# Second layers of a mixture of experts as seven products for eight, with bias rows added by accumulating DMAs

## The chip, the cores and the metric

The kernel runs on one core of a Trainium2 chip. The metric is the device time of one execution in microseconds (us), lower is better. The engines are TensorE (PE in the profile, PEld its weight loads), VectorE (DVE), ScalarE (ACT), GpSimd (POOL) and SyncE (SP). SP and POOL issue the DMAs here: those of SP are in the hardware queue, those of POOL in the software queue, and only POOL's can accumulate, that is, add what they bring to what lies at the destination.

## The reference

One block on x of 2 x 512 tokens by 1024 features. Both quantised factors are rounded to eight bits, all else is float32:

```
x = x + tanh(g_xattn) * (fake_quant(layernorm(x)) @ fake_quant(ctx))      # ctx: 1024 x 1024 for each batch
n = layernorm(x)
scores = softmax(n @ router_w + router_b) + router_bias                   # 16 experts, 2 chosen for each token
z = (silu(n @ sw1 + sb1) * (n @ sw2 + sb2)) @ sw3 + sb3                   # shared expert, 512 hidden
y = sum over experts e: gate[e] * ((silu(n @ ew1[e] + eb1[e]) * (n @ ew2[e] + eb2[e])) @ ew3[e] + eb3[e])   # 256 hidden
out = x + tanh(g_ffn) * (y + z)
```

With the inputs given all tokens choose the same two experts, and the kernel has a path for at most two: there are eight chunks of 128 hidden units, four of the shared expert (chunks 0 to 3) and two of each of the two routed ones (4 to 7). A slower path for any other choice stands behind a branch and doesn't run.

The "first layers" are the products with sw1, sw2, ew1, ew2; the "second layers" the products with sw3 and ew3.

## The kernel before

A float32 product is made on PE from three products of a 32-bit format with fewer bits: each operand is split into a high part (ACT copies it into that format, L333) and a low part (DVE subtracts the high part, L334), and high x high, high x low and low x high are added up in PSUM.

The work comes in this order:
- attention, layer norm, transposes, and the shared expert's chunks 0 to 2 of the first layers, in an order written out by hand (`START`); the router (L638 to L737), whose choice is read into registers, so that weights of chosen experts can be loaded;
- chunk 3 of the shared expert and the four routed chunks (4 to 7), each in a `pair` (names s3, b4, b5, b6, b7): both first layers of a chunk over both batches, as seven products for eight (Winograd's form of Strassen's scheme, 2 x 2 blocks: the halves of the 1024 features, the two batches, the two layers). One product is twelve matmuls of 128x512. The sums of x that it needs (S1 to S4) are made once, by eight accumulating DMAs (`add_x`, L786); the differences of the weights (T's) by `prep_pair` on DVE during the pair before. After each product the caller's `between` step is issued, then what adds the product up (L430 to L452). Routed chunks are multiplied by the tokens' gates on POOL (L421), and the results go to DRAM (`h_all`, L425, POOL's queue);
- the second layers: `load_down` brings back one chunk's hidden units and weights (L862, SP), `split_down` splits them, and `down_mm` (L874, L875, L877) multiplies: for each tile of 128 tokens and each half of the 1024 output columns, all eight chunks add up in one PSUM bank. Three tiles go first, chunk by chunk as chunks arrive; then the other five one by one. x after attention was stored to DRAM (`x_after`) and comes back (`Y`, L908); DVE adds the three bias rows to it, one shared and two routed ones scaled by the tokens' gates (L912), and at last the PSUM banks (`down_end`, L916), and SP stores the tile (L917). The last tile is cut into 512, 256 and 256 columns.

From `manual.enter_context` on, each engine takes its instructions in the order of the program, and so do the two DMA queues: what waits holds up all that stands behind it on that engine or queue. Tiles come from rotating pools: 17 slabs and 14 octs, seven scratch tiles (`temp`), eight PSUM banks. A new tile waits for all users of the one whose place it takes.

Of the kernel before, what the change touches and what calls it, by code (L numbers as in the profile page):

```python
# [9 lines left out]
F32 = mybir.dt.float32  # L10
# [8 lines left out]
P = 128  # L19
D = 1024  # L20
KD = D // P
B = 2
# [57 lines left out]
def flamingo_block(  # L80
# [19 lines left out]
    def slab(name, dtype, shape=(P, D)):  # L100
        return slabs.tile(list(shape), dtype, tag="slab", name=name)
# [20 lines left out]

    X = [None] * NT
    x_after = [spill.tile([P, D], F32, name=f"x_after{t}") for t in range(NT)]
    h_all = [spill.tile([P, B * S], F32, name=f"h_all{c}") for c in range(NC)]


    dq = [nc.sync]
# [170 lines left out]
    def fn(t, h):  # L299
        nm, r = md_[t]  # L300
        nc.vector.tensor_scalar(xn_[t][:, half(h)], X[t][:, half(h)], nm, r, ALU.add, ALU.mult)  # L301
# [30 lines left out]
    def split(raw, hi, lo):  # L332
        nc.scalar.copy(hi, raw)  # L333
        nc.vector.tensor_tensor(lo, raw, hi.bitcast(F32), ALU.subtract)  # L334
        return hi, lo

    def split_in_one(name, raw):

        both = octo(name, F32R, (P, 2, *raw.shape[1:]))
        return split(raw, both[:, 0], both[:, 1])  # L340
# [37 lines left out]
    def prep_pair(name, wa, wb, W):  # L378


        lo, hi = slice(0, KH), slice(KH, KD)
        two = lambda n: tuple(slab(f"{name}{n}{m}", F32R, (P, KD, P)) for m in "hl")
        ah, al = two("a")
        W["B11"], W["B21"] = (ah[:, lo], al[:, lo]), (ah[:, hi], al[:, hi])
        t13, t24 = slab(f"{name}t13", F32, (P, KD, P)), slab(f"{name}t24", F32, (P, KD, P))
        nc.vector.tensor_tensor(t13[:, lo], wa[:, lo], wb[:, lo], ALU.subtract)
        nc.vector.scalar_tensor_tensor(t24[:, lo], t13[:, lo], -1.0, wb[:, hi], ALU.mult, ALU.subtract)
        nc.vector.tensor_tensor(t13[:, hi], wb[:, hi], wb[:, lo], ALU.subtract)
        nc.vector.tensor_tensor(t24[:, hi], wa[:, hi], t24[:, lo], ALU.add)
        split(wa, ah, al)  # L390
        yield
        b22 = slab(f"{name}b22", F32R, (P, KD, P))
        W["B22"] = split(wb[:, hi], b22[:, lo], b22[:, hi])
        yield
        for n, t in (("24", t24), ("13", t13)):
            h, l = split(t, *two(f"t{n}"))
            W[f"T{n[0]}"], W[f"T{n[1]}"] = (h[:, lo], l[:, lo]), (h[:, hi], l[:, hi])
            yield

    def pair(name, W, b1, b2, ci, gates=None, between=()):  # L400


        pa, pb, pc = (bank(f"{name}{n}") for n in "ABC")
# [17 lines left out]
                nc.gpsimd.tensor_tensor(silu, silu, gates[:, ts(b, S)], ALU.mult)  # L421

        def done(h, silu, b):
            nc.vector.tensor_tensor(h, h, silu, ALU.mult)
            nc.gpsimd.dma_start(h_all[ci][:, ts(b, S)], h)  # L425

        s1, s6, s7, s11 = (temp(f"{name}{n}") for n in ("s1", "s6", "s7", "s11"))
        product(pa, "A11", "B11", True)
# [80 lines left out]
    def sup_post(c, b, got, lo=0, n=S):  # L509
        h = up_post(f"sa{c}_{b}_{lo}", got, sb1c(c), sb2c(c), n)  # L510
        nc.sync.dma_start(h_all[c][:, b * S + lo : b * S + lo + n], h)
# [241 lines left out]
    def begin(n, raws):  # L753
        prep[0] = prep_pair(f"b{n}", *raws, W[n])
        next(prep[0])

    def go():
        next(prep[0], None)
# [2 lines left out]
    begin(3, raw3)  # L761
    go()
    go()
    sup_post(0, 1, got, 0, 256)
    go()
    lT = []
# [49 lines left out]
    load_block(SC)  # L816
    for j in range(2):
        nc.sync.dma_start(g_row[j].rearrange("(t p) -> p t", p=P), chosen[j][1])
    f = lambda fn, *a: (lambda: fn(*a))
    pair("s3", W[3], sb1c(3), sb2c(3), 3, None, (  # L820
        [f(split_x, "S1", s1)],
        [f(split_x, "S4", s4)],
        [f(lambda: begin(SC, raws_up[SC]))],
        [go],
        [go],
        [go, f(load_block, SC + 1), f(load_gates, 0)],
    ))
    down_prep = []
    for n in range(SC, NC):
        j, c = divmod(n - SC, EC)  # L830
        bv = chosen[j][2]
        if n + 1 < NC:
            between = (
                [f(begin, n + 1, raws_up[n + 1])], [], [go], [go], [go], [],
                [f(load_block, n + 2)] if n + 2 < NC else [],
            )
        else:
            between = down_prep
        if c == 0 and j == 1:
            load_gates(1)  # L840
        if n == NC - 1:
            break
        pair(f"b{n}", W[n], bv[:, 0, c : c + 1], bv[:, 1, c : c + 1], n, gates[j], between)


    def expert_row(w, e, c=None):
        if c is None:
            return w[ds(e, 1), :].rearrange("o d -> (o d)").partition_broadcast(P)
        return w[ds(e, 1), ts(c, P), :].rearrange("o p d -> (o p) d")

    def w3_rows(c):
        if c < SC:
            return sw3[ts(c, P), :]
        j, c = divmod(c - SC, EC)
        return expert_row(ew3, chosen[j][0], c)

    hid, w3, raw_down = [], [], {}

    def load_down(c):
        raw_down[c] = slab(f"h{c}r", F32), slab(f"d{c}r", F32)  # L860
        for raw, src in zip(raw_down[c], (h_all[c], w3_rows(c))):
            nc.sync.dma_start(raw, src)  # L862

    def split_down(c):
        for n, raw, got in zip("hd", raw_down[c], (hid, w3)):
            if c == 0:
                got.append(split(raw, *(slab(f"{n}{c}{m}", F32R) for m in "hl")))
            else:
                got.append(split_in_one(f"{n}{c}", raw))

    def down_mm(po, t, c, cols):
        (hh, hl), (wh, wl) = hid[c], w3[c]
        for p, cl in zip(po, cols):
            nc.tensor.matmul(p, hh[:, ts(t, P)], wh[:, cl], start=c == 0, stop=False)  # L874
            nc.tensor.matmul(p, hh[:, ts(t, P)], wl[:, cl], start=False, stop=False)  # L875
        for p, cl in zip(po, cols):
            nc.tensor.matmul(p, hl[:, ts(t, P)], wh[:, cl], start=False, stop=c == NC - 1)  # L877

    def bias_row(name, row):
        bb = slab(name, F32)  # L880
        dq[0].dma_start(bb, row)
        return bb

    n, bv = NC - 1, chosen[1][2]
    load_down(0)
    pair(f"b{n}", W[n], bv[:, 0, 1:2], bv[:, 1, 1:2], n, gates[1], (
        [f(load_down, 1)],
        [f(split_down, 0), f(load_down, 2)],
        [f(split_down, 1)],
        [f(split_down, 2), f(load_down, 3)],  # L890
        [f(split_down, 3), f(load_down, 4)],
        [f(split_down, 4), f(load_down, 5)],
        [f(load_down, 6)],
    ))

    gt = rt("gt", (P, 2, NT))
    for j in range(2):
        nc.vector.tensor_scalar(gt[:, j], chosen[j][1], tgf, None, ALU.mult)
    rows = []

    def load_rows():
        rows.append((bias_row("sb", sb3.partition_broadcast(P)), lambda t: tgf))
        for j in range(2):
            rows.append((bias_row(f"eb{j}", expert_row(eb3, chosen[j][0])), lambda t, j=j: gt[:, j, t : t + 1]))

    def down_load(t):
        X[t] = slab(f"Y{t}", F32)
        nc.sync.dma_start(X[t], x_after[t])  # L908

    def down_bias(t):  # L910
        for bb, scale in rows:
            nc.vector.scalar_tensor_tensor(X[t], bb, scale(t), X[t], ALU.mult, ALU.add)  # L912

    def down_end(po, t, cols):
        for p, cl in zip(po, cols):
            nc.vector.scalar_tensor_tensor(X[t][:, cl], p, tgf, X[t][:, cl], ALU.mult, ALU.add)  # L916
            nc.sync.dma_start(of[ts(t, P), cl], X[t][:, cl])  # L917

    halves = [half(0), half(1)]
    first, rest, last = (4, 5, 6), (7, 0, 1, 2), 3  # L920
    po = {t: [bank(f"po{t}_{h}") for h in range(2)] for t in first}
    for c in range(NC):
        if c == 0:
            split_down(5)
        if c == 1:
            load_down(7)
            split_down(6)
        if c == 2:
            split_down(7)
            load_rows()  # L930
            for t in first:
                down_load(t)
        if c == 4:
            for t in first:
                down_bias(t)
        for t in first:
            down_mm(po[t], t, c, halves)
    for t in first:
        down_end(po[t], t, halves)
    order = (*rest, last)  # L940
    for t in order[:2]:
        down_load(t)
    for n, t in enumerate(rest):
        down_bias(t)
        po = [bank(f"po{t}_{h}") for h in range(2)]
        for c in range(NC):
            down_mm(po, t, c, halves)
        down_end(po, t, halves)
        if n + 2 < len(order):
            down_load(order[n + 2])  # L950
    down_bias(last)
    for cl in (slice(0, 512), slice(512, 768), slice(768, 1024)):
        po = [bank(f"po{last}_{cl.start}")[:, : cl.stop - cl.start]]
        for c in range(NC):
            down_mm(po, last, c, [cl])
        down_end(po, last, [cl])
    manual.close()


# [47 lines left out]
                xl(t, h)  # L1007

    def mlp(name, n, up, down, b1, b2, row, scale):
        bb = bias_row(f"{name}bias", row)  # L1010
        for t in range(NT):
            nc.vector.scalar_tensor_tensor(X[t], bb, scale(t), X[t], ALU.mult, ALU.add)
        for c in range(n):
# [97 lines left out]
```

## Time and profile before

| what | before |
|---|---|
| time, median of 3 (lowest, highest) | 322.97 us (322.70, 323.48) |
| profiled execution: its own time, its span | 323.01 us, 321.3 us |
| granted PE clock, mean | 0.994 |
| pair b7 begins | 208.61 us |
| first matmul of the second layers | 228.24 us |
| last addition on DVE begins | 316.30 us |
| DMA: moved, mean rate over the span | 53.44 MB, 166 GB/s |
| of that hardware queue, software queue | 46.27 MB, 6.82 MB |
| accumulating DMAs (L786) | 8 of 512 KB |

Times inside the profile count from the span's start. "Share" of DMA is the mean busy share of the core's 16 DMA engines. A group "L916 DVE ... xcount" is all instructions of one line and shape, with their mean duration. The chain of waits names, going back from the last instruction, what ended last at each step.

### The profile page before, as it was taken

The page shows a single profiled execution, that of the slowest core. Times are in us where ns is not written, and L with a number is a line of the kernel's source. Part 1 is how long each engine was busy: PE and PEld are TensorE (multiplying, and loading weights), DVE is VectorE, ACT ScalarE, POOL GpSimd, SP SyncE. Part 2 cuts the span into 40 slices and gives each one's busy share as a digit, 9 for nine tenths or more (in the row PEclk, how much of TensorE's full clock was granted, in tenths as well). Part 3 has the DMA queues.
Part 4 walks back from the last instruction along what each step waited for, and adds up shares of the span by engine and source line. Part 5 has one row for each costly group of instructions (what it writes and reads, how often), then busy time and mean ns, then how long its engine had stood idle before and what let it go on. Part 6 is the DMA issues. An engine that isn't in the chain of part 4 may idle for free.

```text
span 321.3 us, 4424 instructions
## 1 busy us (share of the span) xinstructions
PE 306.1 (95%) x1626; PEld 244.9 (76%) x1631; DVE 218.8 (68%) x360; ACT 116.2 (36%) x176; POOL 88.7 (28%) x130
## 2 busy tenths in 40 slices
PE   8588799999999999999999999999999999999993
PEld 2244695869995988888888888887788888888883
DVE  3869999997476886396657546479762975663261
ACT  2666669676545307361323324057610000000000
POOL 2695678896900322000013131112200000000000
PEclk9799999999999999999999999999999999999999
DMA  6999992029210999246341604459569053332121
GB/s 207 421 380 358 418 313 111 2 81 343 68 34 18 179 184 208 77 94 149 115 128 66 192 36 149 147 196 337 208 210 356 5 195 131 132 131 74 59 98 41
DMA packets 35105, 53.44 MB, mean 166 GB/s; under 512 B 5436, under 2 KB 23172, under 8 KB 35076
## 3 DMA queue, kind: packets, MB, share of 16 engines
q1 hardware_dynamic: 33124, 46.27, 42.0%
q0 software_dynamic: 1952, 6.82, 8.7%
q8 instruction: 15, 0.25, 0.3%
q14 instruction: 14, 0.11, 0.1%
HBM read 36.29 MB, written 12.59 MB: 152 GB/s over the span
## 4 chain that ended last, share of the span: by engine, by line
PE 83%; DVE 4%; DMA 4%; POOL 4%; issue 2%; ACT 2%; SPq 0%; DVEq 0%; POOLq 0%
PE sp L549 11%; PE sp L360 10%; PE po L877 9%; PE po L874 9%; PE po L875 9%; PE at L251 5%; PE b4B L410 3%; PE b6B L410 3%; PE b5B L410 3%; PE s3B L410 3%; DMA h4r<-h_all 2%; DMA X<-in_dram 2%; PE px L306 2%; PE b7A L410 2%; PE b5C L410 2%
## 5 line engine op out<-in xcount | busy, mean ns | idle before, releaser
L875 PE MATMUL po<-d,h 128*128 128x512 f32 (+1 forms) x119 | 44.9, 377 | 0.0
L874 PE MATMUL po<-d,h 128*128 128x512 f32 (+1 forms) x119 | 44.9, 377 | 0.0
L877 PE MATMUL po<-d,h 128*128 128x512 f32 (+1 forms) x119 | 36.9, 377 | 0.0
L251 PE MATMUL at<-cq,qT 128*128 128x512 bf16 x123 | 29.7, 379 | 2.9 <-POOL cq L170 1.7
L916 DVE SCALAR_TENSOR_TENSOR Y<-po,tg,Y 128x512 f32<-128x512 f32 (+1 forms) x17 | 11.4, 715 | 21.4 <-PE po L877 21.3
L875 PEld LDWEIGHTS po<-d,h 128*128 128x128 f32 x119 | 22.4, 188 | 4.1
L874 PEld LDWEIGHTS po<-d,h 128*128 128x128 f32 x119 | 22.4, 188 | 4.1
L877 PEld LDWEIGHTS po<-d,h 128*128 128x128 f32 x119 | 22.4, 188 | 4.1
L251 PEld LDWEIGHTS <-qT 128*128 128x128 bf16 x128 | 12.1, 97 | 15.7 <-issue 3.0
L912 DVE SCALAR_TENSOR_TENSOR Y<-eb,gt,Y 128x1024 f32<-128x1024 f32 x16 | 20.6, 1285 | 0.6
L912 DVE SCALAR_TENSOR_TENSOR Y<-sb,tg,Y 128x1024 f32<-128x1024 f32 x8 | 10.2, 1278 | 10.3 <-DMA Y<-x_after 10.3
L786 POOL DMA_DIRECT2D xf<-xf x8 | 7.2, 931 | 28.8 <-PE plt L649 15.0
L549 PE MATMUL sp<-XH,sb 128*128 128x256 f32 x96 | 14.1, 292 | 0.0
L549 PE MATMUL sp<-XH,sa 128*128 128x256 f32 x96 | 13.7, 288 | 0.0
L316 DVE TENSOR_TENSOR XL<-px,XH 128x512 fp32r<-128x512 f32 x16 | 10.4, 678 | 3.7 <-ACT xf L323 3.7
L549 PEld LDWEIGHTS sp<-XH,sb 128*128 128x128 f32 x96 | 12.3, 191 | 0.5 <-DVE sb L164 0.2
L360 PE MATMUL sp<-XH,sa 128*128 128x256 f32 (+1 forms) x64 | 12.5, 338 | 0.0
L360 PE MATMUL sp<-XH,sb 128*128 128x256 f32 (+1 forms) x64 | 12.5, 338 | 0.0
L549 PEld LDWEIGHTS sp<-XH,sa 128*128 128x128 f32 x96 | 12.3, 192 | 0.1
L272 ACT ACTIVATE xn<-X,s 128x512 f32<-128x512 f32 x16 | 11.4, 716 | 2.1 <-DVE X L263 1.8
L301 DVE TENSOR_SCALAR xn<-X,nm,d 128x512 f32<-128x512 f32 x16 | 11.2, 726 | 1.4 <-POOL d L297 1.3
L183 DVE BATCH_NORM_STATS2 st<-X 128x6 f32<-128x512 f32 x16 | 10.3, 680 | 2.3 <-DMA X<-in_dram 2.3
(499 smaller groups left out, 690.6 us busy)
## 6 DMA issues: line engine op xcount, KB each, us to landing
cr<-in_dram SPq DMA_DIRECT2D x15, 512.0 KB, 9.9
x_after<-X SPq DMA_DIRECT2D x8, 512.0 KB, 4.3
xf<-xf POOLq DMA_DIRECT2D x8, 512.0 KB, 5.1
Y<-x_after SPq DMA_DIRECT2D x8, 512.0 KB, 5.3
out_dram<-Y SPq DMA_DIRECT2D x15, 256.0 KB, 2.0
X<-in_dram SPq DMA_DIRECT2D x7, 512.0 KB, 9.0
h_all<-sa SPq DMA_DIRECT2D x8, 128.0 KB, 1.8
gates<-g_row SPq DMA_DIRECT2D x2, 512.0 KB, 5.3
```

The costliest lines, as they stand in the source:

```text
L251: nc.tensor.matmul(acc[t][h], qT[b][:, t % TB, k, :], cq[b][k // KH][:, k % KH, half(h)], start=(k == 0), stop=(k == KD - 1))
L272: nc.scalar.activation(xn_[t][:, half(h)], X[t][:, half(h)], AF.Square, bias=s[:, h : h + 1], scale=-float(H), accum_out=q[:, h : h + 1],)
L301: nc.vector.tensor_scalar(xn_[t][:, half(h)], X[t][:, half(h)], nm, r, ALU.add, ALU.mult)
L316: nc.vector.tensor_tensor(XL[b][q][p], px_[t, q], XH[b][q][p].bitcast(F32), ALU.subtract)
L360: nc.tensor.matmul(p, wx[:, k, :], xx[b][k // KH][:, k % KH, cols], start=first and k == 0, stop=last and k == KD - 1,)
L410: nc.tensor.matmul(p, w[:, k, :], x[:, k, :], start=f and k == 0, stop=l and k == KH - 1, skip_group_check=not first,)
L549: nc.tensor.matmul(up_[c, lo, i], w[:, k, :], x[0][k // KH][:, k % KH, lo : lo + 256], start=p == 0 and k == 0, stop=p == 2 and k == KD - 1,)
L874: nc.tensor.matmul(p, hh[:, ts(t, P)], wh[:, cl], start=c == 0, stop=False)
L875: nc.tensor.matmul(p, hh[:, ts(t, P)], wl[:, cl], start=False, stop=False)
L877: nc.tensor.matmul(p, hl[:, ts(t, P)], wh[:, cl], start=False, stop=c == NC - 1)
L912: nc.vector.scalar_tensor_tensor(X[t], bb, scale(t), X[t], ALU.mult, ALU.add)
L916: nc.vector.scalar_tensor_tensor(X[t][:, cl], p, tgf, X[t][:, cl], ALU.mult, ALU.add)
```

## The change

The second layers become one 2 x 2 block product, in seven products for eight: the hidden units are cut into shared (512) and routed (512) and into the two batches, the weights into shared and routed rows and the two halves of the columns. With `A11`, `A12` = shared and routed hidden units of batch 0, `A21`, `A22` of batch 1, and `B11`, `B12`, `B21`, `B22` the weights (shared rows first), the sums are S1 = A21 + A22, S2 = S1 - A11, S3 = A11 - A21, S4 = A12 - S2, T1 = B12 - B11, T2 = B22 - T1, T3 = B22 - B12, T4 = T2 - B21 (with a sign taken into the code: `nS3`, `nT3`, `T4` as B21 - T2). Products are made in four groups of 128 tokens, each twelve matmuls of 128x512, in the order A11 B11, A12 B21, S2 T2, nS3 nT3, A22 T4, S1 T1, S4 B22.

- The first product is needed in both batches' sums: ACT copies its PSUM banks to four others, on which later products add up.
- The sums of hidden units are made by accumulating DMAs from DRAM (`add_part`, POOL's queue) on a tile that ACT wrote; the differences of weights by DVE in place (`less`).
- After each product but the first, DVE adds its PSUM banks to `Y` (`down_add`); the 24 additions of 512 columns (the last one cut in two) are spread over six products, where before there were two of them for each tile at its end.
- Bias rows: the two routed ones are scaled and summed for each token tile and half (`sum_rows`, ACT and DVE) during pairs b4 to b6, and added to `x_after` in DRAM by 16 accumulating DMAs of 256 KB (`add_sum`, POOL). The shared row is scaled by ACT once and added to each loaded `Y` by an accumulating DMA of 512 KB (`add_row`, POOL), eight in all. DVE's 24 bias additions go.
- `done` stores hidden units through SP's queue instead of POOL's.
- `prep_pair` works in place in the raw weights and is spread over one step more.

```diff
-    h_all = [spill.tile([P, B * S], F32, name=f"h_all{c}") for c in range(NC)]
+    h_dram = [spill.tile([P, KH, B * S], F32, name=f"h{n}") for n in ("shared", "routed")]
+    h_all = [h_dram[c // SC][:, c % SC] for c in range(NC)]
...
-            nc.vector.tensor_tensor(h, h, silu, ALU.mult)
-            nc.gpsimd.dma_start(h_all[ci][:, ts(b, S)], h)
+            got = keep[0] if keep and b == 0 else h
+            nc.vector.tensor_tensor(got, h, silu, ALU.mult)
+            nc.sync.dma_start(h_all[ci][:, ts(b, S)], got)
...
+    def sum_rows(h, t):
+        u = sums[h, t] = temp(f"u{h}_{t}")
+        nc.scalar.mul(u, rows[h][:, 0], gt[:, 0, t : t + 1])
+        nc.vector.scalar_tensor_tensor(u, rows[h][:, 1], gt[:, 1, t : t + 1], u, ALU.mult, ALU.add)
+
+    def add_sum(h, t):
+        nc.gpsimd.dma_start(x_after[t][:, half(h)], sums[h, t], accum_op=ALU.add)
...
+    def add_part(name, part, *at, parts=(0, 1)):
+        for i in parts:
+            nc.gpsimd.dma_start(R[name][i], part(*at, i), accum_op=ALU.add)
...
+    def down_mm(p, t, a, b, first, cl=slice(None)):
+        for k in range(KH):
+            (ah, al), (bh, bl) = ((m[k // 2][:, k % 2] for m in (HI[n], LO[n])) for n in (a, b))
+            for i, (x, w) in enumerate(((ah, bh), (ah, bl), (al, bh))):
+                nc.tensor.matmul(
+                    p, x[:, ts(t, P)], w[:, cl], start=first and k == 0 and i == 0, stop=k == KH - 1 and i == 2,
+                    skip_group_check=not first,
+                )
+
+    def down_load(t):
+        X[t] = slab(f"Y{t}", F32)
+        nc.sync.dma_start(X[t], x_after[t])
+
+    def add_row(t):
+        nc.gpsimd.dma_start(X[t], rows["s"], accum_op=ALU.add)
+
+    def down_add(p, t, h, store, cl=None):
+        cl = half(h) if cl is None else slice(h * H + cl.start, h * H + cl.stop)
+        nc.vector.scalar_tensor_tensor(X[t][:, cl], p, tgf, X[t][:, cl], ALU.mult, ALU.add)
+        if store:
+            nc.sync.dma_start(of[ts(t, P), cl], X[t][:, cl])
...
+    def product(p, a, b, first, post, meanwhile):
+        for t, steps in zip(range(TB), meanwhile):
+            down_mm(p[t], t, a, b, first)
+            post(t)
+            for step in steps:
+                step()
+
+    high("A12", parts=two)
+    low("A12", parts=two)
+    scaled("S2", "nS3", 1.0)
+    add_part("S2", h_part, 1, 1)
+    for t in range(TB):
+        down_load(t)
+        add_row(t)
...
+    product(pa, "A11", "B11", True, lambda t: nc.scalar.copy(pb[t], pa[t]), (
...
+    fetch("A22", h_part, 1, 1)
+    fetch("S1", h_part, 0, 1)
+    add_part("S1", h_part, 1, 1)
+    product(pa, "A12", "B21", False, lambda t: down_add(pa[t], t, 0, True), (
+        [f(high, "S2"), f(low, "S2", parts=one)],
+        [f(low, "S2", parts=two), f(scaled, "S4", "S2", -1.0), f(add_part, "S4", h_part, 1, 0)],
...
+    product(pb, "S2", "T2", False, lambda t: down_add(pb[t], t, 1, False), (
...
+    for t in range(TB, NT):
+        down_load(t)
+        add_row(t)
+    fetch("B22b", w3_part, 1, 1)
+    product(pb, "nS3", "nT3", False, lambda t: down_add(pb[t], TB + t, 1, False), (
+        [f(low, "T4", parts=two)], [f(high, "A22"), f(low, "A22", parts=one)], [f(low, "A22", parts=two)],
+        [f(high, "S1"), f(low, "S1", parts=one)],
+    ))
+    product(pb, "A22", "T4", False, lambda t: down_add(pb[t], TB + t, 0, True), (
...
+    product(pc, "S1", "T1", True, lambda t: down_add(pc[t], TB + t, 1, True), (
...
+    product(pc, "S4", "B22b", False, lambda t: down_add(pc[t], t, 1, True), [[]] * (TB - 1))
+    for cl in (slice(0, 256), slice(256, 512)):
+        down_mm(pc[TB - 1][:, cl], TB - 1, "S4", "B22b", False, cl)
+        down_add(pc[TB - 1][:, cl], TB - 1, 1, True, cl)
```

`fetch` loads a block through SP, `high` and `low` make its two parts (ACT and DVE), `scaled` multiplies a block by a number on ACT. Operands of the first two products are loaded and split in the steps of pair b7.

## The prediction

> **What bounds the kernel now.** I read the page's busy table first, then the chain of waits in order of time, then busy time by stretches, and last the transfers. The profiled execution took 323.01 us with a span of 321.3, so 1.7 us lie around the span; the median is 322.97, so its profile stands for the median. A difference under about 0.3% (1 us) can't be told from no change here.
>
> ```profile
> PE 306.1 (95%) x1626; PEld 244.9 (76%) x1631; DVE 218.8 (68%) x360; ACT 116.2 (36%) x176; POOL 88.7 (28%) x130
> ```
> ```profile
> 208.61 2.72 PE b7A L410 x12
> 211.33 2.72 PE b7B L410 x12
> ...
> 231.12 0.61 DVE b7s L452
> ...
> 231.77 0.50 PE po L874
> ...
> 316.30 0.48 DVE Y L916
> ```
> ```profile
> 109.00:111.55 2.55, 2.55 (x18) 2.33 (x18) 2.21 (x12) 0.00 (x0) 0.86 (x1) 1.00 0.98 193
> 111.55:115.75 4.20, 4.20 (x21) 3.46 (x20) 3.79 (x13) 0.00 (x0) 0.86 (x2) 1.00 1.03 204
> 245.00:247.00 2.00, 2.00 (x11) 1.65 (x10) 0.00 (x0) 0.00 (x0) 0.00 (x0) 1.00 1.03 418
> 227.60:321.30 93.70, 88.46 (x412) 73.77 (x410) 51.44 (x53) 6.61 (x7) 2.41 (x3) 1.00 0.35 129
> 10.00:14.00 4.00, 2.82 (x10) 1.22 (x11) 3.50 (x7) 3.25 (x5) 3.39 (x8) 0.57 1.03 421
> ```
> TensorE (PE) is the bound. In the chain, a product of the first layers is twelve 128x512 matmuls in 2.72 us, 0.227 us each, and pairs follow one another every 19.04 us. The second layers run from 228 to 316 with nothing late but a 0.2 us wait at 231.77 for DVE. In the stretches (columns: bounds, length, busy us of PE, PEld, DVE, ACT, POOL, then PE clock, DMA share, GB/s) the second layers use DVE little over half and DMA 0.35. The first two stretches hold the eight accumulating transfers of L786: 512 KB each, alone, they fill the DMA engines (0.98, 1.03) at 193 to 204 GB/s. The third holds plain loads: the engines are as full at 418. So an accumulating transfer costs the engines twice a plain one: 2.6 us per 512 KB against 1.3 (at 200 and 400 GB/s).
>
> **The change, part by part.**
>
> *TensorE.* Before: 8 chunks x 8 token tiles x 2 halves x 3 = 384 matmuls. After: 7 products x 4 tiles x 12 = 336. 28 groups of twelve at 2.72 are 76.2 us, and some 0.2 for the last group cut into 256 columns. b7 begins at 208.61 and has seven products, so the second layers can begin at 227.65 and end at 304.0; the last DVE addition then starts at 304.2 instead of 316.30. If nothing waits, that is 12.1 us less: 310.9 us.
>
> *DVE, ACT.* Gone are 24 bias additions of 1.28 us on DVE; PE never waited for them, so they give nothing. New are, per product, four additions of 0.75 (L916), four low parts of 1.22 (L334) and up to two differences of some 1.2: 7.9 to 10.3 us of a product's 10.88. It fits, but DVE runs in order: one operand that comes late stops the low parts behind it. ACT has four high parts of 1.05 a product, the four PSUM copies and sums. The PSUM-to-PSUM copy has no row; PSUM to SBUF took 0.59 (L430), so 0.3 to 1.2, I take 0.6. By the order on ACT they run at 234 to 242, and the second product's first group overwrites the first copied bank from 238.5; nothing is late by either end. In the pairs, 16 sums of routed rows add 0.69 on DVE and 0.6 on ACT each, at most six a pair: DVE goes from 12.0 (its rows of pair b5) to some 16 of 19.04. The new order of `prep_pair` has the same operations one product later, finished before the next pair. Cost 0 for these.
>
> *Queues.* The ten hidden-layer stores move from POOL to SP, where what is behind waits too: the Y0 load stands behind b7's last store. That waits for: product 6's end at 224.93, addition 0.69, silu 0.72, gate 1.30, multiply 0.69, one low part 1.22, addition and multiply 1.38, near 231. Y0 to Y3 and 2 MB of hidden rows (A22, S1) leave SP from 231.4, some 0.4 us apart. On POOL the accumulations of S2 go at 233 (after two ACT parts), then the row additions of Y0 to Y3, S1, S4, then Y4 to Y7: each in this order.
>
> *DMA, where I see the loss.* From 232 the engines have work without a gap. Product 4 adds to Y4 to Y7, and each addition waits for its accumulated row. On DVE, Y6's addition stands ahead of the second low part of A22, and product 5's first group needs that at its ninth matmul. Unstalled, product 5 begins at 227.65 + 4 x 10.88 = 271.2 and that matmul at 273.0; less 1.22 and 0.75, Y6's row must have landed at 271.0. Ahead of it and with it are:
> - accumulating: S2, S1, S4 1 MB each, Y0 to Y6 0.5 each: 6.5 MB x 5.24 us = 34.1;
> - plain: Y0 to Y7 4 MB, A22 and S1 2, four half tiles stored 1, the last weights (B22b) 1: 8 MB x 2.62 = 21.0.
>
> Together 55.1 us from 232, and some 1.2 from the last byte to the wait's end (transfers of L786, issued in pairs, landed 4.5 to 6.5 us after issue): 288.3. The order between the two queues hardly matters, as the plain ones have all been issued by 262. Then 0.75 and 1.22, and four matmuls more: the group ends at 291.2 against 273.9, 17.3 late. Earlier waits (product 3 for S2's low part behind Y1's row, some 3 us) are inside that. PE has then stood nearly idle from 274 to 290. At the start, where it had waited 2.93 us, the granted clock was 0.57 over 4 us (last stretch): 4 x 0.43 = 1.7 more. Sum: 310.9 + 17.3 + 1.7 = 329.9, say 330.
>
> *The unknown prices.* S2, S1 and S4 accumulate from DRAM in 2 KB pieces; the trace has accumulation from SBUF in 4 KB pieces only. I take the same 2.6 per 512 KB, the nearest row. As cheap as plain copies, 3 MB come 7.9 cheaper: 322.0. Half as dear again: 337.8. The routed sums accumulate into DRAM (16 x 256 KB, no such row): 1.3 each by that row, 21 us over three pairs whose DMA share is about half; I take 0 for their delay. At three times that, b7's scratch tiles, which wait for the accumulation issued near 209, would hold PE up to 5 us. A gain here I exclude: nothing was waiting.
>
> *What the Trainium skill says.* "DMA: Bandwidth & Descriptors", section "Anatomy of one DMA — SWDGE (gpsimd) path", fits any transfer from GpSimd as 2.0 us and its bytes at 436 GB/s, without a word on accumulation. By it the 6.5 MB would be an estimated 15.6 us of engine time, the sum 36.6 after 232, Y6 in time, and the change worth its 12.1 us. The stretches at 193 to 204 GB/s speak against it, and I go by them. Against the change speaks the same page's section "Queues, rings and completion order": an engine takes its queues in turn, packet by packet, so that plain and accumulating packets would wait for each other; no row of this trace has the two together for long.
>
> **Rivals.**
> 1. *Faster: plain copies ride inside accumulations.* If an accumulating packet only waits for its second read, the engine could move plain packets meanwhile. Place: the same wait of DVE for Y4 to Y7. Up to 271.0 there are 271.0 - 232 - 1.2 = 37.8 us for 34.1 of accumulation, so it decides at 3.7 us: with no more than that charged for the 21.0 of plain copies, product 5 waits for nothing, and it is 310.9; with half charged, 6.8 late, some 318. For it: the mix is not in the trace. Against it: shares of 0.98 and 1.03 in both kinds, never the sum of two. 310.9 to 319.
> 2. *Near no change: accumulation from DRAM at the plain price.* 322.0 as above, 319 to 324 with the landing times. Against it: an accumulation reads two operands wherever they lie, and 200 is half of 400.
> 3. *Slower still: accumulation into DRAM holds the pairs* (b5 to b7), as priced: 335 to 342. For it: no row shows this kind. Against it: at the price taken, its 21 us of engine time have three pairs, 57 us, to fit in.
>
> That the change doesn't do what it says I set aside: the order of PE's instructions shows the 336 matmuls.
>
> **How the numbers follow.** Forecast (late row additions, near 330; own range 323 to 337): 0.62. Rival 1: 0.23. Rival 2: 0.10. Rival 3: 0.05. Faster is rival 1 and half of rival 2: 0.28. Same is 0.04, from rival 2's middle; slower the rest, 0.68. The range must take in most of rival 1 as well: 313 to 337; it leaves out rival 3's far half, the edges, and rival 1's unstalled end.
>
> **What would show it.** Right: PE's products at 2.72 us per group; DVE waiting for Y's rows with software transfers as releaser, longest before product 5's operands; PE nearly idle for over 10 us between products 4 and 5; DMA share near 1 from 232 to 288 with 250 to 300 GB/s; a clock under 1 after it. Wrong: PE without a wait through 28 groups (rival 1), a first wait of DVE for Y0 under 1 us, or PE waits inside b6 or b7 (rival 3). A span under 316 refutes the DMA sum; products at another pace than 2.72 refute the first term.

## The result, and the profile after

The changed kernel takes 343.86 us (median of 4, 342.40 to 345.49); the kernel before, beside it, 323.23. The ratio is 1.0639, interval 1.0583 to 1.0694: slower by 6.4%. Medians are of all executions; the ratios and their intervals leave out those over 1.5% above the kernel's fastest. The forecast was slower, near 330.0 and at most 337: the direction held, the size did not. The profiled execution took 342.40 us with a span of 340.6, 12.5 us more than the forecast.

The busy table of the kernel after:

```profile
PE 303.9 (89%) x1566; PEld 239.5 (70%) x1571; DVE 231.9 (68%) x380; ACT 147.7 (43%) x215; POOL 113.8 (33%) x152
```

PE has 60 instructions less than before, but is busy for 2.2 us less only, and its share falls from 95% to 89%. So it waits, and what it does takes longer. The waits of PE (us in total, times, longest), those of the second layers:

```profile
PE pb L921 <- DVE Y L935: 7.1, 1, 7.1
PE pb L921 <- DVE S2l L904: 5.2, 2, 4.1
...
PE pa L921 <- ACT pb L1003: 3.7, 1, 3.7
PE pb L921 <- DVE A22l L904: 2.8, 1, 2.8
```

The chain of waits from pair b7 on (start, length, what):

```profile
210.56 2.72 PE b7A L412 x12
...
236.50 1.30 POOL b7s L423
...
248.60 15.48 DMA Y<-rows
...
264.84 1.23 DVE S2l L904
...
266.11 6.04 PE pb L921 x16
...
272.41 10.07 DMA Y<-x_after
...
283.03 14.56 DMA Y<-rows
...
298.35 1.23 DVE A22l L904
...
299.62 13.18 PE pb L921 x46
312.80 20.48 PE pc L921 x96
```

Pair b7 begins 2 us late. Its second gate runs at 236.50. The shared row's accumulation into Y, alone 2.6 us of engine time, takes some 15 us from issue to landing, twice in the chain. DVE adds to Y only then, and makes the low parts of S2 and A22 behind that. Product 5 goes on in the PSUM banks of product 4, so its first matmul waits until the addition to Y4 has read its bank: this is the longest wait, 7.1 us. From 299.62 on PE waits for 0.6 us only.

Busy time by stretches (bounds, length, then PE, PEld, DVE, ACT, POOL, then granted clock, DMA share, GB/s): the second layers from their first matmul to the last addition, the end of b6 and b7, and the stretch of the late rows:

```profile
229.72:335.60 105.88, 86.32 (x349) 68.63 (x347) 56.53 (x61) 30.15 (x33) 15.53 (x15) 0.87 0.75 202
205.00:232.00 27.00, 27.00 (x120) 22.04 (x119) 15.07 (x17) 10.79 (x13) 9.51 (x10) 1.00 1.04 279
240.00:297.60 57.60, 40.70 (x150) 31.17 (x148) 30.28 (x31) 21.69 (x25) 14.24 (x14) 0.83 1.03 266
```

The DMA engines are full (1.03) from 240 to 297.6, as forecast for 232 to 288, but they were full before that too: 1.04 from 205 to 232, where the forecast had room. In the first line PE is busy for 86.32 us on work of 76.4 (28 groups at 2.72 us and the cut of the last), at a clock of 0.87.

### The profile page after: what moved, and what is told of

Same layout as the page of the kernel before. It is cut to its first block, busy times and chain, and to the rows that moved or that the text cites. A ratio compares the mean times of both kernels' runs of the same rounds, so it can differ in the third digit from the quotient of the medians.

```text
span 340.6 us, 4476 instructions
## 1 busy us (share of the span) xinstructions
PE 303.9 (89%) x1566; PEld 239.5 (70%) x1571; DVE 231.9 (68%) x380; ACT 147.7 (43%) x215; POOL 113.8 (33%) x152
## 4 chain that ended last, share of the span: by engine, by line
PE 51%; DMA 25%; issue 10%; SPq 5%; DVE 4%; POOL 2%; ACT 2%; POOLq 0%; DVEq 0%; ACTq 0%
PE sp L552 10%; DMA Y<-rows 9%; PE sp L364 8%; PE pc L921 7%; PE pb L921 6%; DMA cr<-in_dram 5%; DMA e0a1r<-in_dram 4%; PE at L252 4%; DMA Y<-x_after 3%; DMA x_after<-u 2%; PE px L307 2%; PE b6B L412 2%; PE b4B L412 2%; PE b5A L412 2%; PE b7A L412 2%
## 5 line engine op out<-in xcount | busy, mean ns | idle before, releaser
L935 DVE SCALAR_TENSOR_TENSOR Y<-pb,tg,Y 128x512 f32<-128x512 f32 x12 | 9.0, 749 | 18.9 <-DMA Y<-rows 16.3
L853 POOL DMA_DIRECT2D x_after<-u x16 | 14.0, 949 | 10.5 <-DVE u L850 10.5
L423 POOL TENSOR_TENSOR b4s<-b4s,gates 128x512 f32<-128x512 f32 x2 | 2.8, 1396 | 43.9 <-ACT b4s L439 36.3
L849 ACT ACTIVATE u<-row,gt 128x512 f32<-128x512 f32 x16 | 11.3, 721 | 9.1 <-DMA x_after<-u 6.1
L892 POOL DMA_DIRECT2D rS<-hrouted x6 | 7.3, 1505 | 22.1 <-DMA rS<-hshared 14.9
L935 DVE SCALAR_TENSOR_TENSOR Y<-pc,tg,Y 128x512 f32<-128x512 f32 (+1 forms) x9 | 6.2, 691 | 11.7 <-PE pc L921 11.7
L921 PE MATMUL pb<-T4h,A22h 128*128 128x512 f32 x16 | 7.6, 473 | 7.1 <-DVE Y L935 7.1
L552 PE MATMUL sp<-XH,sa 128*128 128x256 f32 x96 | 13.7, 287 | 0.0
L850 DVE SCALAR_TENSOR_TENSOR u<-row,gt,u 128x512 f32<-128x512 f32 x16 | 11.7, 746 | 1.3 <-ACT u L849 1.0
L364 PE MATMUL sp<-XH,sa 128*128 128x256 f32 (+1 forms) x64 | 12.5, 338 | 0.0
L364 PE MATMUL sp<-XH,sb 128*128 128x256 f32 (+1 forms) x64 | 12.5, 337 | 0.0
L921 PE MATMUL pb<-T2h,S2l 128*128 128x512 f32 x16 | 7.6, 473 | 5.2 <-DVE S2l L904 5.2
```

The costliest lines, as they stand in the source:

```text
L364: nc.tensor.matmul(p, wx[:, k, :], xx[b][k // KH][:, k % KH, cols], start=first and k == 0, stop=last and k == KD - 1,)
L552: nc.tensor.matmul(up_[c, lo, i], w[:, k, :], x[0][k // KH][:, k % KH, lo : lo + 256], start=p == 0 and k == 0, stop=p == 2 and k == KD - 1,)
L849: nc.scalar.mul(u, rows[h][:, 0], gt[:, 0, t : t + 1])
L850: nc.vector.scalar_tensor_tensor(u, rows[h][:, 1], gt[:, 1, t : t + 1], u, ALU.mult, ALU.add)
L853: nc.gpsimd.dma_start(x_after[t][:, half(h)], sums[h, t], accum_op=ALU.add)
L921: nc.tensor.matmul(p, x[:, ts(t, P)], w[:, cl], start=first and k == 0 and i == 0, stop=k == KH - 1 and i == 2, skip_group_check=not first,)
```

## The experiments

Theory A, from the prediction: accumulating transfers fill the DMA engines, Y's rows land late, and DVE, in order, holds the operands behind them. Theory B: the loss is made before the second layers, by the routed sums. Beside each group the kernel before ran on the same chip, at 323.2 to 323.5 us.

### Which accumulations cost what

**No shared row.** `add_row` does nothing.

```diff
-        nc.gpsimd.dma_start(X[t], rows["s"], accum_op=ALU.add)
+        pass
```

> Leaves the shared bias row out of the output: the eight 512 KB accumulations into Y are gone, all else stays. Theory A (the row accumulations fill the DMA engines, so Y and the operands behind it on DVE come late): 4 MB at 5.24 us/MB = 21 us of engine time go, PE's 19 us of idle time between 240 and 306 us nearly vanish; what stays is the late start (the gate of b7 at 236.5 instead of 226.5): 317 to 324 us. Theory B (the loss is made before b7 ends, by the routed sums that hold the loads of A12 and the scratch tiles): over 332 us.

Measured: 322.14 us, ratio 0.9938 [0.9906, 0.9969]; 21.7 less than after. Theory A's value. Its longest waits in the second layers are 3.1 us for the PSUM copy and 1.5 for S2's high part: the late start is still there (gate of b7 at 238.81).

**No routed sums.** `add_sum` does nothing.

```diff
-        nc.gpsimd.dma_start(x_after[t][:, half(h)], sums[h, t], accum_op=ALU.add)
+        pass
```

> Leaves the routed bias rows out of the output: the sixteen 256 KB accumulations into x_after in DRAM are gone, their sums on ACT and DVE stay, all else stays. Theory A: b7 begins 1 to 2 us sooner, A12 lands before its high part is due, Y0 to Y3 leave SP about 10 us sooner, but the 55 us of engine time from 232 us on stay: about 330 us, the price worked out before. Theory B: under 322 us.

Measured: 334.72 us, ratio 1.0351 [1.0306, 1.0396]; 9.1 less than after. Between the two, nearer to A: B alone falls, but these transfers, taken at no delay in the prediction, cost 9.1 us. This kernel is the case that the prediction's sum described; Y's loads leave SP from 232.19 here. PE's waits, and DVE's additions to Y4, Y5 and Y6 behind the accumulated rows:

```profile
PE pb L921 <- DVE Y L935: 9.5, 1, 9.5
PE pb L921 <- DVE S2l L904: 4.7, 2, 3.3
...
PE pb L921 <- DVE A22l L904: 2.7, 1, 2.7
```
```profile
285.74 0.75 DVE L935 SCALAR_TENSOR_TENSOR Y<-pb,tg,Y 128x512 f32<-128x512 f32 x1 [14.08 <-DMA Y<-rows]
...
288.62 0.75 DVE L935 SCALAR_TENSOR_TENSOR Y<-pb,tg,Y 128x512 f32<-128x512 f32 x1 [0.99 <-DMA Y<-rows]
...
291.09 0.75 DVE L935 SCALAR_TENSOR_TENSOR Y<-pb,tg,Y 128x512 f32<-128x512 f32 x1 [0.59 <-DMA Y<-rows]
```

The sum had the row of Y6 landed at 288.3; its addition starts at 291.09, and in the kernel after at 300.35.

**Neither.** Both edits.

> Leaves all bias rows out of the output: neither the sixteen accumulations into x_after nor the eight into Y. The seven products alone, with the sums of hidden rows by DMA left. If the PE term of the prediction holds (28 groups of 2.72 us from 227.65 us): 311 to 314 us. If the sums of hidden rows (3 MB accumulating) or the order on ACT and DVE hold PE by themselves: over 317 us.

Measured: 312.87 us, ratio 0.9691 [0.9633, 0.9749]; 31.0 less than after, where the two single losses add up to 30.8. The stretch of its second layers, with the columns as above:

```profile
226.56:303.90 77.34, 76.72 (x349) 63.68 (x347) 54.68 (x59) 27.86 (x30) 7.77 (x7) 1.00 0.70 206
```

PE is busy for 76.72 of 77.34 us: the seven products, with the sums of hidden units, the PSUM copy and DVE's additions beside them, are worth 10 us against the kernel before. The bias rows cost 31, and so take back three times that.

### Engine time or order

**The row copied, not added.** Same place, source, size and waits.

```diff
-        nc.gpsimd.dma_start(X[t], rows["s"], accum_op=ALU.add)
+        nc.gpsimd.dma_start(X[t], rows["s"])
```

> The eight row transfers into Y keep their place, source, size and waits, but copy and do not add, so that Y holds the shared row in place of x and the routed rows. Theory A (an accumulating 512 KB takes the DMA engines 2.6 us, a plain one 1.3): half of the 21 us of engine time stays; the loss without the row transfers was 21.7 us smaller, so some 11 us smaller here: 331 to 335 us. Rival (it is the order of issue and the wait for each load that cost, whatever the transfer does): within 3 us of 343.9.

Measured: 333.90 us, ratio 1.0353 [1.0305, 1.0401]: 10.0 of the 21.7 us come back with nothing changed but the addition. In the trace a packet of this transfer, 4 KB, takes 327 ns where it adds and 159 where it copies.

**The routed sums copied, not added.**

```diff
-        nc.gpsimd.dma_start(x_after[t][:, half(h)], sums[h, t], accum_op=ALU.add)
+        nc.gpsimd.dma_start(x_after[t][:, half(h)], sums[h, t])
```

> The sixteen transfers of the routed sums into x in DRAM copy and do not add, so that x is lost there; all else as after. The loss without them was 9.1 us smaller. If it is engine time (178 ns of a 2 KB accumulating packet against 84 to 89 of a plain one): about half comes back, 338 to 341 us. If it is their place in the queues and the waits for them: within 2 us of 343.9.

Measured: 336.32 us, ratio 1.0426 [1.0359, 1.0493]: 7.5 of the 9.1 come back, more than the half expected, so engine time again. Adding, they go in packets of 2 KB at 210 ns in the mean; copying, of 4 KB at 170: 1.7 us of the engines for 256 KB against 0.7. ACT now waits 3.1 us for A12, not 10.5.

**A12's parts behind b7's silu.**

```diff
-    last[5] += [f(high, "A12", parts=one), f(low, "A12", parts=one), f(fetch, "B22", w3_part, 1, 1, buf=in_slabs)]
+    last[5] += [f(fetch, "B22", w3_part, 1, 1, buf=in_slabs)]
-    last[6] += [f(high, "B21"), f(low, "B21", parts=one)]
+    last[6] += [f(high, "B21"), f(low, "B21", parts=one), f(high, "A12", parts=one)]
...
+    low("A12", parts=one)
     high("A12", parts=two)
```

> Computes everything; on ACT the high part of the first half of A12 goes behind the last silu of b7, and its low part on DVE behind b7's last multiplication. Theory A2 (the late load of A12 costs its time through the order on ACT: the silu behind it, then b7's gate, store and the Y loads, come 10 us late): the gate starts near 226.5, Y0 to Y3 leave SP near 232, and of the 9 us that the routed sums cost some 7 come back: 335 to 338 us. Rival (the DMA engines are full from 205 on, so the work only waits elsewhere): over 341 us.

Measured: 338.49 us, ratio 1.0477 [1.0444, 1.0509]: 5.4 back, just outside the 335 to 338 of theory A2 and well away from the rival. The gate of b7 on POOL, in the kernel after and then here:

```profile
236.50 1.29 POOL L423 TENSOR_TENSOR b7s<-b7s,gates 128x512 f32<-128x512 f32 x1 [13.12 <-ACT b7s L450]
```
```profile
228.74 1.29 POOL L423 TENSOR_TENSOR b7s<-b7s,gates 128x512 f32<-128x512 f32 x1 [5.38 <-ACT b7s L450]
```

So the path of the routed sums is mostly this: they fill the DMA engines in b6 and b7, A12's load takes 13 us, ACT waits for it with b7's silu behind it, and gate, store and the Y loads (which leave SP from 241.45) come some 8 us late.

**The routed rows' load later.** Its packets of 2 KB took about 1 us each from 140 to 149 us, and 84 ns elsewhere.

```diff
-        [f(split_x, "S4", s4), f(load_rows, 0)],
+        [f(split_x, "S4", s4)],
...
-        [go, f(load_block, SC + 1), f(load_gates, 0)],
+        [go, f(load_block, SC + 1), f(load_gates, 0), f(load_rows, 0)],
```

> Computes everything; the load of the first half of the routed rows moves from behind the 2,048 four-byte stores of the gates (139 us) to some 10 us later. If the slow packets (near 1 us for 2 KB) belong to the place behind those stores, the row packets fall to 0.1 to 0.2 us, other loads there crawl as in the kernel before, and b4 and b5 begin 1 to 2 us sooner: 341 to 343 us. If they belong to reading one row for 128 partitions, they stay near 1 us at the new place, and the time is the same or longer.

Measured: 344.28 us, ratio 1.0661 [1.0607, 1.0716]: no gain, where 341 to 343 was expected. The point on the packets held: the row packets fall to about 0.1 us, and weight packets of 512 B, now in that place, take 166 ns in the mean (141 to 149 us), where 27 is usual. What crawls is the place behind the four-byte stores; why it does was not tried.

### Other ways to add the rows

**The shared row on GpSimd.**

```diff
-        nc.gpsimd.dma_start(X[t], rows["s"], accum_op=ALU.add)
+        nc.gpsimd.tensor_tensor(X[t], X[t], rows["s"], ALU.add)
```

> Computes everything: the shared row is added to each Y by one 128x1024 addition on GpSimd in place of an accumulating DMA. Theory A: the DMA engines lose the same 21 us as without the row, GpSimd gets 8 x about 2.6 us (twice its 1.30 us for 128x512) of some 100 us: within 2 us of the kernel without the row. Rival (the place in GpSimd's queue, not the engine time, makes Y late: S1 and S4 wait behind Y's loads in either form): over 5 us above the kernel without the row.

Measured: 331.87 us, ratio 1.0248 [1.0158, 1.0339]: 9.7 above the kernel without the row. The size is the rival's, the reason is neither's. The lines of the weight differences on DVE (durations in ns: least, median, most) with the additions on GpSimd, and the additions themselves, then the differences in the kernel without the row:

```profile
L915 DVE TENSOR_TENSOR rB<-rB,rB x8: 1211/2288/3416, 243.7 to 274.8; 128x1024 f32<-128x1024 f32 x8
...
L931 POOL TENSOR_TENSOR Y<-Y,rows x8: 2395/3336/3397, 245.6 to 285.9; 128x1024 f32<-128x1024 f32 x8
```
```profile
L915 DVE TENSOR_TENSOR rB<-rB,rB x8: 1212/1217/1220, 246.7 to 272.6; 128x1024 f32<-128x1024 f32 x8
```

While GpSimd adds, a DVE subtraction takes up to 3.4 us for 1.2. The Trainium skill, "SBUF — State Buffer", section "Who interferes with whom", says that a DVE instruction with two inputs in SBUF contends with a GpSimd instruction that reads SBUF; this pair of rows agrees.

**The shared row on DVE**, half by half, in `down_add` ahead of that half's first addition from PSUM; `add_row` does nothing.

```diff
+        if (t, h) not in rows:
+            rows[t, h] = True
+            nc.vector.tensor_tensor(X[t][:, cl], X[t][:, cl], rows["s"][:, cl], ALU.add)
```

> Computes everything: the shared row is added to each half of Y by a 128x512 addition on DVE (16, about 0.69 us each) right ahead of that half's first output addition, in place of the accumulating DMAs. DVE gets 2.8 us more in each of products 2 to 5, against 7.9 to 10.3 of 10.88. If what made the same additions on GpSimd cost 9.7 us over the kernel without the row is that DVE ran at a third of its pace while GpSimd added: here 322 to 327 us, below the 331.9 of GpSimd. If any such addition holds the products as much: 330 or more.

Measured: 325.85 us (321.34 to 331.42, n = 10), ratio 1.0014 [0.9971, 1.0056]: as fast as the kernel before, and by the medians 6 us under the additions on GpSimd. With this alone the change would have been worth nothing, and lost nothing.

**All rows on PE.** Gates (and 1 for the shared row) and rows lie as high and low parts on 67 partitions; one matmul more per output tile and half adds all three rows in PSUM. No row goes by DMA into Y or x, no sums on ACT and DVE.

```diff
+    def bias_mm(p, t, n, h, cl=slice(0, H)):
+        nc.tensor.matmul(
+            p, rows[n][:KB, ts(t, P)], rows["R"][:KB, h * H + cl.start : h * H + cl.stop], start=False, stop=True,
+            skip_group_check=True,
+        )
...
             down_mm(p[t], t, a, b, first)
+            if bias:
+                bias_mm(p[t], t, *bias)
```

`bias` is given for the last product that each output half has to itself: products 2, 5 and 6, and 7 with the difference of two batches' gates, since product 6's bank goes on into product 7.

> Computes everything: no bias row goes by DMA or DVE any more; one matmul more for each output tile and half (67 partitions: gates and rows as high and low parts) adds all three rows in PSUM. From the kernel without any row (312.9) plus 16 x 0.227 = 3.6 us of PE: 316.5 us, 315 to 319, under the kernel before. If the small transfers of gates and rows or the new operations on ACT, DVE and GpSimd hold a pair: up to 322.

Measured: 317.79 us, ratio 0.9834 [0.9810, 0.9859]: faster than the kernel before by 1.7%, and than the changed one by 26 us. Part of its chain of waits:

```profile
242.66 2.73 PE pa L928 x12
245.63 2.73 PE pa L928 x12
248.59 2.73 PE pa L928 x12
251.56 24.50 PE pb L928 x108
```

A group with the row takes 2.97 us from start to start, 0.25 more than one without; 16 of them are the 4 us between this kernel and the one without rows, with 0.9 left over.

## Why the prediction was right, and where it failed

Two terms of the sum failed: the delay of the routed sums, put at 0, cost 9.1 us, and the clock, charged 1.7 us for one stall, cost 8.9. They overlap, since the delay brings more stalls at half clock.

**PE term: right.** From the first matmul to the last addition 76.55 us were forecast; without bias rows it is 77.34, and the whole 312.87 against 310.9. With them, the second layers begin at 229.72 instead of 227.65: 2.1 us late.

**DVE, ACT and the copy at no cost: right as far as sizes go.** A PSUM copy takes 0.57 us (0.6 taken), and nothing waits for it without the bias rows. What the step missed is order on ACT: it said that a late operand stops what is behind it on DVE, and did not look for the same on ACT, where A12's high part stands ahead of b7's silu.

**Queues: wrong.** Y's loads were to leave SP from 231.4; they left from 241.45, but from 232.19 without the routed sums. The place in the queue was right, the time of what was ahead was not.

**The DMA sum: right in total for the case it was made for, not in its place.** PE was to stand for 17.3 us, and without the routed sums it is idle for 17.5 (98.58 us less 81.06 busy). But the row of Y6 came some 2.7 us later than the sum had it, and PE did not wait for it at product 5's ninth matmul: it waited 9.5 us at the first, for the PSUM bank that the addition to Y4 still had to read, 2.7 for the low part of A22 behind Y5, and 4.7 in product 3. The prediction did not have the wait for the bank, so that the totals agree so closely is partly luck. In the kernel after it is 19.6 (105.88 less 86.32).

**Unknown prices: the one taken at zero was not zero.** Accumulation from DRAM takes 176 ns a packet of 2 KB, 2.8 us for 512 KB; 2.6 was taken. Into DRAM a packet takes 210 ns in the mean, 1.7 us for 256 KB (128 packets over 16 engines) for 1.3 taken. But their delay was put at nothing because the share of before was half in those pairs; with the operand loads of the second layers there too, it is 1.04 from 205 to 232, and the kernel without them is 9.1 us faster. Rival 3 named this transfer and priced 335 to 342, at a chance of 0.05 only; the place it gave, scratch tiles that hold PE, is the small part of it: pair b7 begins 2 us late.

**The clock: the term that was mis-sized.** One stall was to cost 1.7 us. In the kernel after PE is busy for 86.32 us on work of 76.4: 9.9 us more. There are three stretches at half the full clock, of 6.8, 6.8 and 13.7 us, begun by the waits at 241, 259 and 288:

```profile
243.33:250.16 6.83, 5.66 (x13) 4.45 (x14) 6.83 (x7) 2.08 (x4) 4.17 (x4) 0.50 1.00 302
263.81:270.64 6.83, 5.73 (x15) 3.94 (x14) 3.77 (x4) 3.89 (x4) 1.21 (x1) 0.50 1.04 263
291.12:304.77 13.65, 6.34 (x14) 4.32 (x15) 7.59 (x9) 5.78 (x6) 0.00 (x0) 0.50 0.80 170
```

PE is busy for 17.7 us of them, and half of that, 8.9 us, is the clock's part of the 9.9. Without routed sums there is one of 17.1 us, 10.0 of it idle, and PE is busy for 4.7 us more than its work. The step took one row from the kernel's start, 0.57 over 4 us, and charged one stall; the forecast's own "some 3 us" before product 3 it did not charge, and the wait for the PSUM copy, 3.7 us, it did not have.

The Trainium skill, "TensorE: Matmul & The Clock Gate", section "What's actually happening", has the array at half rate after an idle window of about 3.4 us, and the windows running on whatever the kernel does. The traces agree on the windows: the stretches are 3.41 us or a multiple of it, and in each execution all begin on one grid of 3.41 us. They do not agree that a window must be idle throughout. In all twelve kernels' traces from 225 us on, each of the 21 full-clock windows of that grid with PE idle for 1.91 us or more (by the profile, which models the ends of matmuls) was followed by half clock, and none of those with 1.80 or less was. So what a wait of about 3 us costs depends on how it falls on the grid. Of a wait of 2.9 us with the row on DVE, 1.91 fell into one window (first two lines: the window, and the next at half clock); one of 3.1 without the shared row was split into 1.3 and 1.8, and brought no half clock (last two):

```profile
244.57:247.98 3.41, 1.50 (x6) 1.24 (x7) 3.41 (x4) 2.82 (x5) 2.44 (x2) 1.00 0.97 219
247.98:251.39 3.41, 3.41 (x10) 2.63 (x8) 3.41 (x4) 0.00 (x0) 0.00 (x0) 0.50 1.03 363
```
```profile
245.01:248.42 3.41, 1.60 (x7) 1.35 (x8) 3.41 (x4) 2.72 (x5) 2.44 (x2) 1.00 0.86 202
248.42:251.83 3.41, 3.41 (x17) 2.83 (x16) 3.41 (x4) 0.00 (x0) 0.00 (x0) 1.00 1.04 369
```

Together: 2.1 of a late start, 2.3 more idle, and 8.2 more of busy time beyond the work are 12.6 of the 12.5 us between forecast and profile. Against the kernel without routed sums, which begins its second layers at 228.17, the three are 1.6, 2.0 and 5.3: most of what the routed sums cost is half clock.

**The rivals.** Rival 1 (plain copies ride inside accumulations) falls: with both kinds mixed for 57 us the engines show 1.03 at 266 GB/s, between the 200 and 400 of the pure stretches, and making the row's transfers plain gave half of their cost back. Rival 2 falls by the 176 ns. That "slower" held rests on theory A, which removals and halvings of both transfers bear out: without the routed sums the change is still 3.5% slower. Not tried: A12's load at an earlier place in SP's queue, and routed sums that carry the shared row as well.

## What to carry to other kernels

Price an accumulating transfer at twice its bytes or somewhat more, and add up engine time in every stage that issues or waits for transfers, not only in the one where the loss is expected. When a sum of work ends in stalls of PE, charge each stall that can take some 2 us out of one window of 3.41 us its own stretch at half clock. A rank-3 addition of rows that an idle engine or the DMA is to hide may be cheapest on the engine that is the bound: here 17 short matmuls, 4 us of PE, took the place of transfers and additions that had cost 31.

## What was not expected of the hardware

- The 2,048 four-byte stores of the gates take 9 ns a packet and are all but through by 141 us, but what is loaded next crawls for some 8 us: the DMA engines move 19 GB/s from 142 to 146 us and 16 from 146 to 150. From 141 to 149 us a packet of 2 KB takes 1.1 us in the mean for 84 ns. In the kernel before, where nothing waited for those loads, packets of 512 B take 107 ns in the mean for 27. Slow packets are not the whole of it: with the row on DVE most 2 KB packets there take 81 ns, and the engines move 6 and 11 GB/s all the same.
- Additions of 128x1024 on GpSimd take 3.3 us each beside DVE's subtractions and 2.4 at the least, and DVE's then take up to 3.4 for 1.2: both lose. DVE is busy for 244.6 us in all with the additions on GpSimd and for 241.6 with them on DVE itself, so work moved to an "idle" GpSimd can cost DVE more than the work.
- A matmul over 67 partitions costs what one over 128 does: 0.24 us for 512 columns against 0.227.
